# A conditional residual and paged attention on one core: written order on all engines, a queue of norms with fixed slots, and the sets in the order q01, kv, q23

## The chip, the core and the metric

The kernel runs on one core of a Trainium2 chip. The metric is the device time of one execution in microseconds; lower is better. The core has five engines, each with a queue of its own: TensorE (PE, with its weight load PEld), VectorE (DVE), ScalarE (ACT), GpSimd (POOL) and SyncE (SP). SP issues most of the DMAs, POOL the gathers of V and some stores, ACT a few stores.

## What is computed

The input x is 64 batches of 32 tokens of 512 values. All is float32.

```
W = L0_cond_weights[condition]                     # 64 x 32 x 32
x = x + einsum('bct,bcd->bdt', x, W)               # x1
q, k, v = x1 @ Wq.T, x1 @ Wk.T, x1 @ Wv.T          # 32 heads of q, 8 of k and v, 128 wide
q, k = rope(rmsnorm(q) * q_norm_w), rope(rmsnorm(k) * k_norm_w)
k_all = concat(k_cache[block_table], k)            # 512 cached rows (16 pages of 32), 32 new ones
v_all = concat(v_cache[block_table], v)
probs = softmax(mask(q @ k_all.T / sqrt(128)))     # cached rows beyond the length are masked
out = x1 + (probs @ v_all) @ Wo.T
```

## The kernel before, in words

**Tiling.** Four batches (4 x 32 = 128 tokens) make a *step*. There are 16 tiles of four batches, and the heads are taken in two halves (`hh`): steps 0 to 15 compute four key heads with their sixteen query heads, steps 16 to 31 the others. Within a step each batch `bt` has four *slots*, one for each key head `g`; slot = 4 bt + g, so a step has sixteen slots, 0 to 15. The main loop runs over steps, batches and key heads.

**What a slot holds.** `scores` (L800) multiplies the cached keys of one head by the queries of four heads (eight matmuls in L804) and ACT takes the exponential (`pr`, L815). `values` (L859) multiplies the exponentials of the slot before by V (L865); DVE adds the part of the new keys, takes the reciprocal and scales (L883 to L886), and `turn` transposes the result (L896). `head_keys` (L788) copies the keys of one head out of the loaded pages (`kh`, L797, DVE), three heads ahead; there are three `kh` tiles. `next_values` (L1266) masks one block of gathered V rows on ACT (L361) and issues a gather three blocks ahead on POOL (L348). At slot 0 `new_scores` multiplies the new keys by the queries (`psn`, L825) and ACT makes `pn` (L833); at slots 1 and 3 `new_values` multiplies `pn` by the new V (`pnv`, L849) and ACT copies it. At the start of each batch SP issues the sixteen K pages of the batch after next (L321); for the last batch of a step eight at its start (slot 12) and eight at slot 13.

**Work for later steps.** Between these, the slots carry the projections for the step after next. Steps 1 to 3 are projected plainly (`classic`). From step 4 on two steps form a *pair*, and their projections are made by a Strassen-like scheme of seven products for a *set* of weights: set 0 is q heads 0 and 1 (q01), set 1 is q heads 2 and 3 (q23), set 2 is k and v (kv). The products of a set are in four pieces (`products`, L655; the matmuls are L665, the sums on DVE L681, the first copy `z` on ACT L695), and a table `where` (L1214) gives the slots of each: for pair steps n + 2 and n + 3, set 0 in slots 4, 6, 8, 9 of step n, set 1 in slots 11 to 14 of step n, and set 2 in slots 4, 6, 8, 11 of step n + 1; n is even. Sums of weights are made once for each half (`sums_w`), stored, and loaded again (`load_sums`, L652). Each product that is a query or key head goes through `finish` to `norm_rope` (L465): a Square on ACT (L470), the mean on DVE (L474, L475), a power on POOL (L477), five DVE operations (L481 to L496), then a transpose on DVE and a store of the rows to DRAM on POOL's queue (`turn_rows`, L512 to L520). `spread` (L522) loads the rows as columns for the step that uses them: `q_cols` for batches 0 to 2, `q_last` for batch 3. `out_proj` (L736) multiplies the outputs of the step before by the output weights (L743), in four parts; `reload` and `store` bring and take the accumulated tile.

**Order.** `plan` and `ahead` are tables of work by (step, slot) and (step, batch), filled by `at`, `input_of`, `set_of`, `spread_of`, `angles_of` and `tables_of`. For PE and SP the order is the written one during the whole kernel (`manual_schedule`, L91). For DVE, ACT and POOL it is the written one until `opening.close()` (L1109); after that a planner with a cost model orders their instructions, but for those that `tc.issue_after` ties to an earlier one (L1146, L1269). The planner's order is fixed in the program; nothing is reordered at run time.

**Tiles.** The accumulated tile (`x1_a`, L375) is in tag `acc` with two buffers, or in `sums` or `u3`. `z`, `u2`, `u3`, `w1`, `w2` are single buffers of sums and norms. PSUM has two banks for scores, two for values and four for all else (`pp`).

Of the kernel before, what the change touches and what calls it, by code (L numbers as in the profile page):

```python
# [20 lines left out]
P = 128  # L21
# [38 lines left out]
def cond_resid_paged_attention_kernel(  # L60
# [148 lines left out]
    def steps_of(exact, pools):  # L209
# [165 lines left out]
        def x1_a(st):  # L375

            tag = "acc"
            if st.n in (2, 3, 5) and not exact:
                tag = "sums"
            elif st.n > 6 and st.n % 2 and not exact:  # L380
                tag = "u3"
            st.acc = work.tile(
                [P, HID], F32, tag=tag, name=f"acc_{st.name}", bufs=1 if tag[0] == "u" else 2
            )
            src = acc_d[st.t] if st.hh else x[st.t * P : (st.t + 1) * P, :]
            nc.sync.dma_start(st.acc, src)
# [31 lines left out]
        def keep_x1(st):  # L418
            nc.sync.dma_start(acc_d[st.t], st.acc)
# [12 lines left out]
        def rot_tile(st, kind):  # L432
            table = work.tile([P, 2, 2, HD], F32, tag="rot", name=f"rot_{kind}_{st.name}", bufs=2)
            st.rot[kind] = table
            return table
# [29 lines left out]
        def norm_rope(st, pp, name, kind, to=None):  # L465
# [3 lines left out]
            sq = work.tile([P, 4, D], F32, tag="w2", name=f"sq_{name}", bufs=1)  # L469
            nc.scalar.activation(  # L470
                sq.rearrange("p h d -> p (h d)"), pp, AF.Square, scale=1.0 / math.sqrt(D)
# [7 lines left out]
            r = work.tile([P, 4, 2, HD], F32, tag="w1", name=f"rope_{name}", bufs=1)  # L479
            u = work.tile([P, 4, 2, HD], F32, tag="w2", name=f"ropeu_{name}", bufs=1)  # L480
            nc.vector.tensor_tensor(  # L481
                r.rearrange("p h e f -> p h (e f)"),
                pp.rearrange("p (h d) -> p h d", h=4),
                cw.rearrange("p e f -> p (e f)").unsqueeze(1).to_broadcast([P, 4, D]),
                ALU.mult,
            )
# [23 lines left out]
        kept = []  # L510
# [24 lines left out]

        def finish(st, i, pp, name, kind):

            if by_tensor(st):
# [12 lines left out]
                norm_rope(st, pp, name, kind, to)  # L551
            else:
                turn_rows(st, i, norm_rope(st, pp, name, kind))
# [60 lines left out]
        def sums_x(pair):  # L614
            a = lambda i: pair.x[:, i].rearrange("p c q -> p (c q)")
            nc.vector.tensor_tensor(a(S1), a(A21), a(A22), ALU.add)
            nc.vector.tensor_tensor(a(S2), a(S1), a(A11), ALU.subtract)
            nc.vector.tensor_tensor(a(S4), a(A12), a(S2), ALU.subtract)
            nc.vector.tensor_tensor(a(S3), a(A11), a(A21), ALU.subtract)
# [35 lines left out]
        def products(pair, k, first):  # L655
# [46 lines left out]
            def p5_p2():  # L702
                t["c"] = bank("pc")
                product(t["c"], S1, t[1], True)
                product(t["a"], A12, t["b21"])
                done(s0, e0, t["a"])

            def p7():
                product(t["b"], S3, made[pair.hh, k][1] if first else pair.t[k, 1])
                t["u3"] = temp("u3")  # L710
                add(t["u3"], t["b"], t["z"])
                if e1[0] == "v":
                    p4 = lambda a: a.rearrange("p (g d) -> p g d", g=GH)
                    add(new_v(s1), p4(t["u3"]), p4(t["c"]))
                else:
                    add(t["u3"], t["c"], t["u3"])
                    done(s1, e1, t["u3"])

            def p4_p3():
# [4 lines left out]
                product(t["c"], S4, t["b22"])  # L724
                if e1[0] == "v":
                    p4 = lambda a: a.rearrange("p (g d) -> p g d", g=GH)
                    add(new_v(s0), p4(t["u2"]), p4(t["c"]))
                else:
                    add(t["u2"], t["c"], t["u2"])
                done(s1, e0, t["z"])  # L730
                if e1[0] != "v":
                    done(s0, e1, t["u2"])

            return p1_p6, p5_p2, p7, p4_p3
# [25 lines left out]
        def reload(st):  # L760
            st.acc = work.tile([P, HID], F32, tag="acc", name=f"res_{st.name}", bufs=2)
# [328 lines left out]
        x1_b(second)  # L1090
        head_keys(later, 0, nc.scalar)
# [17 lines left out]
        opening.close()  # L1109
# [18 lines left out]
        def input_of(st, n, load, weights, mix, turned_at):  # L1128
            at(weights[0], weights[1], lambda: load_cond_weights(st.t))
            at(load[0], load[1], lambda: x1_a(st))  # L1130
# [3 lines left out]
        def set_of(pair, k, n, slots, first):  # L1134
            for slot, work_of in zip(slots, products(pair, k, first)):
                at(n, slot, work_of)

        def spread_of(st, last_cols):
            ahead[st.n - 1, BT - 1].append(lambda: spread(st, 0, BT - 1))
            at(st.n - 1, last_cols, lambda: spread(st, BT - 1, BT))  # L1140

        def angles_of(m, n, slot):
            def angles():
                tmp = work.tile([P, 3, TRIG * HD], F32, tag="w1", name=f"ang{m}", bufs=1)
                with tc.issue_after(last["dve"]), tc.issue_after(last["act"]):
                    reduced(m * TRIG, tmp)  # L1146
                    sines(new_trig(m * TRIG), tmp)
# [28 lines left out]
        spread_of(steps[2], 14)  # L1176
        at(2, 13, lambda: spread(steps[3], 0, BT - 1))
        at(2, 14, lambda: spread(steps[3], BT - 1, BT))


        for pair in pairs:
            s0, s1 = pair.both
            n = s0.n - 2
            early, half_first = n == 2, s0.n == NT
            if early:
                at(2, 3, lambda pair=pair: pair_x(pair))
                input_of(s0, 2, (1, 15), (1, 15), 4, 5)
                input_of(s1, 2, (2, 4), (2, 2), 6, 7)
# [4 lines left out]
            elif not pair.hh:  # L1193
                at(n - 1, 12, lambda pair=pair: pair_x(pair))
                input_of(s0, n - 1, (n - 1, 9), (n - 1, 6), 12, 13)
                input_of(s1, n - 1, (n - 1, 11 if n > 4 else 12), (n - 1, 7), 14, 15)
                at(n, 1, lambda pair=pair: sums_x(pair))
# [228 lines left out]
```

## Time and profile before

| | |
|---|---|
| median of 3 runs | 2268.01 us (2267.06 to 2268.45) |
| profiled execution | 2280.09 us, span of its instructions 2278.3 us |
| mean granted TensorE clock | 0.971 |
| busy share of PE, DVE, POOL, ACT | 94%, 60%, 41%, 38% |
| moved by DMA | 478.65 MB, mean 210 GB/s |

The span runs from the first to the last instruction. A line of a profile names the engine, the line of the kernel, the operation, what is written and read (out<-in), and how often; "idle before" is the time in which the engine stood just before such an instruction, with what ended it. PEclk is the granted TensorE clock as a share of full speed.

### The profile page before, as it was taken

What the parts mean: (1) busy time and instruction counts of PE and PEld (TensorE: products, weight loads), DVE (VectorE), ACT (ScalarE), POOL (GpSimd) and SP (SyncE); (2) the same over time, 40 slices, a digit from 0 to 9 for tenths busy, and PEclk for the clock granted to TensorE, in tenths of its full rate; (3) what the DMA queues carried; (4) which work ended last, traced back from release to release, by engine and by line L of the source; (5) the groups of instructions that cost most, each with busy time, mean ns of one, the idle gap of its engine ahead of it and who ended that gap; (6) DMA issues with size and microseconds to landing.
All of it is one profiled execution on the core that took longest, in us unless ns stands there. A gap on an engine that the chain in (4) does not pass through costs nothing. (4 is left out here: it accounts for less than half of the span.)

```text
span 2278.3 us, 42030 instructions
## 1 busy us (share of the span) xinstructions
PE 2137.4 (94%) x12804; PEld 1507.2 (66%) x12804; DVE 1361.4 (60%) x3142; ACT 865.2 (38%) x1591; POOL 923.3 (41%) x1089
## 2 busy tenths in 40 slices
PE   8998898999999999999999899999999999999998
PEld 4765666676666666666666566676767667676786
DVE  5566674756657566575755646556475565757532
ACT  3533233443433424433333333343333334342452
POOL 4444353534435344353433423334343343434431
PEclk9999899999999999999999999999999999999999
DMA  8775567777677776797757887677777767777673
GB/s 242 200 192 160 175 197 209 222 217 223 192 208 225 208 223 195 209 283 236 214 180 219 237 228 220 196 220 221 216 211 211 219 200 228 216 226 222 184 223 95
DMA packets 424314, 478.65 MB, mean 210 GB/s; under 512 B 57072, under 2 KB 323696, under 8 KB 424080
## 3 DMA queue, kind: packets, MB, share of 16 engines
q1 hardware_dynamic: 366096, 291.72, 45.0%
q0 software_dynamic: 55088, 180.01, 25.9%
q10 hardware_dynamic: 2896, 4.14, 0.5%
q8 instruction: 105, 1.72, 0.3%
q14 instruction: 129, 1.06, 0.1%
HBM read 406.45 MB, written 69.21 MB: 209 GB/s over the span
## 5 line engine op out<-in xcount | busy, mean ns | idle before, releaser
L348 POOL DMA_INDIRECT raw_x<-in_vc_dram,v_row x512 | 525.1, 1026 | 775.7 <-ACT v_x L361 695.3
L815 ACT ACTIVATE pr_x<-ps_x 128x512 f32<-128x512 f32 x511 | 306.5, 600 | 917.8 <-PE ps_x L804 914.8
L865 PEld LDWEIGHTS po_x<-v_x,pr_x 128*128 128x128 f32 x4088 | 531.2, 196 | 157.2 <-issue 138.4
L865 PE MATMUL po_x<-v_x,pr_x 128*128 128x129 f32 x4088 | 563.6, 282 | 6.2 <-ACT pr_x L815 5.4
L743 PE MATMUL pout_x<-wo_x,ot_x 128*128 128x512 f32 x1024 | 464.0, 597 | 10.3 <-DMA wo_x<-in_wo_dram 10.3
L804 PE MATMUL ps_x<-q_cols_x,kh_x 128*128 128x128 f32 x3064 | 419.6, 281 | 45.3 <-DVE kh_x L797 37.7
L804 PEld LDWEIGHTS ps_x<-q_cols_x,kh_x 128*128 128x128 f32 x3064 | 386.0, 198 | 51.0 <-issue 46.3
L797 DVE COPY kh_x<-k_t_x 128x512 f32<-128x512 f32 x506 | 215.6, 433 | 295.2 <-PE ps_x L804 202.3
L361 ACT ACTIVATE v_x<-raw_x,valid 128x512 f32<-128x512 f32 x512 | 366.6, 721 | 41.0 <-DMA raw_x<-in_vc_dram,v_row 40.8
L743 PEld LDWEIGHTS pout_x<-wo_x,ot_x 128*128 128x128 f32 x1024 | 189.3, 192 | 214.5 <-issue 214.5
L477 POOL TENSOR_TENSOR rs_q_x<-ms_q_x,minus_half 128x4 f32<-128x4 f32 x128 | 144.8, 1131 | 155.2 <-DVE ms_q_x L475 154.5
L665 PE MATMUL pb_x<-t_x,x_x 128*128 128x512 f32 x432 | 203.6, 594 | 0.0
L883 DVE TENSOR_TENSOR nv_x<-po_x,nv_x 128x258 f32<-128x258 f32 x256 | 106.3, 415 | 150.8 <-PE po_x L865 143.9
L520 POOL DMA_DIRECT2D heads_d<-rows_x x150 | 122.4, 816 | 153.7 <-DVE rows_x L516 109.4
L474 DVE TENSOR_REDUCE ms_q_x<-sq_q_x 128x4 f32<-128x512 f32 x128 | 86.6, 676 | 114.9 <-ACT sq_q_x L470 113.7
L804 PE MATMUL ps_x<-q_last_x,kh_x 128*128 128x128 f32 x1024 | 136.1, 276 | 0.0
L681 DVE TENSOR_TENSOR u_x<-pb_x,z_x 128x512 f32<-128x512 f32 x84 | 57.6, 686 | 128.0 <-PE pb_x L665 94.8
L804 PEld LDWEIGHTS ps_x<-q_last_x,kh_x 128*128 128x128 f32 x1024 | 125.5, 193 | 0.0
L665 PEld LDWEIGHTS pb_x<-t_x,x_x 128*128 128x128 f32 x432 | 77.2, 192 | 71.1 <-issue 63.0
L665 PE MATMUL pa_x<-wq_x,x_x 128*128 128x512 f32 x224 | 115.1, 640 | 0.0
L886 DVE TENSOR_TENSOR o_x<-nv_x,rden 128x256 f32<-128x256 f32 x256 | 107.4, 420 | 5.1
L665 PE MATMUL pc_x<-wq_x,x_x 128*128 128x512 f32 x224 | 105.4, 593 | 0.5 <-DVE u_x L681 0.5
(180 smaller groups left out, 2033.0 us busy)
## 6 DMA issues: line engine op xcount, KB each, us to landing
k_t_x<-in_kt_dram SPq DMA_DIRECT2D x2048, 64.0 KB
t_x<-sums_d SPq DMA_DIRECT2D x108, 512.0 KB
heads_d<-rows_x POOLq DMA_DIRECT2D x150, 256.0 KB
q_cols_x<-heads_d SPq DMA_DIRECT2D x120, 240.0 KB
q_last_x<-heads_d SPq DMA_DIRECT2D x120, 80.0 KB
sums_d<-t SPq DMA_DIRECT2D x18, 512.0 KB
raw_x<-in_vc_dram,v_row POOLq DMA_INDIRECT x512
wo_x<-in_wo_dram SPq DMA_DIRECT2D x32, 256.0 KB
```

Source lines behind the costliest of these rows:

```text
L348: nc.gpsimd.indirect_dma_start(out=raw.rearrange("p g d -> p (g d)"), out_offset=None, in_=vc, in_offset=bass.IndirectOffsetOnAxis(ap=v_ro ...
L361: nc.scalar.activation(v_bufs[b % 2][:, c, :, 0:D], raw, AF.Copy, scale=ok)
L477: nc.gpsimd.tensor_tensor(rs, ms, minus_half, ALU.pow)
L520: nc.gpsimd.dma_start(heads_d[st.n][:, :, i, :].rearrange("k p c -> p k c"), part)
L665: nc.tensor.matmul(bank, pair.x[:, i, c, :], w[:, c * 512 : (c + 1) * 512], start=start and c == 0, stop=c == 1, skip_group_check=not start,)
L743: nc.tensor.matmul(st.po, st.ot[:, i, :], wt["o", st.hh, i // 4][:, i % 4, :], start=(i == 0), stop=(i == QH - 1),)
L797: last["dve"] = nc.vector.tensor_copy(k, ba.k_raw[:, :, g, :]).ins
L804: nc.tensor.matmul(ps[:, c, :], ba.k[g][:, c * P : (c + 1) * P], queries(ba, g), start=True, stop=True,)
L815: last["act"] = nc.scalar.activation(pr, ps, AF.Exp, scale=SCALE).ins
L865: nc.tensor.matmul(ba.po[:, g % 2, :], ba.pr[g][:, c, :], ba.v_t[:, c, g, :], start=(c == 0), stop=(c == VC - 1),)
L883: nc.vector.tensor_tensor(t, ba.po, t, ALU.add)
L886: nc.vector.tensor_tensor(ba.o[:, both, :], t[:, :, 0:D], rd.unsqueeze(2).to_broadcast([P, 2, D]), ALU.mult,)
```

## The change

DVE, ACT and POOL keep the written order to the end: `opening.close()` moves from the start of the main loop to its end, and the two `tc.issue_after` fall away. Since the written order now counts, several things are written elsewhere:

- **Norms.** `finish` only puts a product into `outputs_due` when it belongs to a pair. The Square is traced at the end of a slot (`square_next`) and the rest of the norm in the next one (`norm_next`), behind its scores and key copy, in fixed slots (`norm_slots`): 7, 9, 10, 11, 14 of even steps, 2, 7, 9, 10 and 14 (in the second half 12) of odd ones; in steps below 4 any slot takes one. In `norm_rope` the first DVE multiplication stands before the mean.
- **Sets.** kv takes slots 11 to 14 of step n, and q23 slots 4, 6, 8, 11 of step n + 1. In a set P3 moves from the last piece to the third, beside P7, and the sums are grouped anew. The v of the pair's second step is kept in `u3` and copied by ACT at slot 4 of step n + 1 (`late_v`).
- **Key copies.** `head_keys` stands right behind `scores` in its slot, where it stood at the slot's end.
- **Accumulated tile.** Tag `acc` has one buffer and serves step 0 and the reloads; steps 1 to 5 use `sums`, later ones `u2` or `u3` by turns. Step 1's tile is stored on POOL's queue and loaded again.
- **SP's order.** The last columns of `spread` follow the others at the start of batch 3, where they had a slot of their own; loads of x, rotation tables, query, key, value and output weights move by some slots; the final reload moves from slot 10 to 14. Rotation tables have four buffers instead of two, and `sums_x` is in two parts, at slots 2 and 3.

The core of the diff (moves of `tables_of`, `input_of` and `sums_w` by a slot or two, and the edits that only pass `sq` and `late_v` on, are left out):

```diff
-            tag = "acc"
-            if st.n in (2, 3, 5) and not exact:
-                tag = "sums"
-            elif st.n > 6 and st.n % 2 and not exact:
-                tag = "u3"
+            tag, bufs = "acc", 2 if exact else 1
+            if 0 < st.n < 6 and not exact:
+                tag, bufs = "sums", 2
+            elif st.n and not exact:
+                tag = ("u2", "u3")[st.n % 2]
...
         def finish(st, i, pp, name, kind):
 
+            outputs_due.append((st, i, pp, name, kind))
+            while outputs_due and (st.pair is None or not in_slots):
+                square_next()
+                norm_next()
+
+        def square_next():
+            if outputs_due and not squared:
+                _, _, pp, name, _ = outputs_due[0]
+                squared.append(squares(pp, name))
+
+        def norm_next():
+            if squared:
+                st, i, pp, name, kind = outputs_due.pop(0)
+                normed(st, i, pp, name, kind, squared.pop())
...
             def p5_p2():
                 t["c"] = bank("pc")
                 product(t["c"], S1, t[1], True)
+                t["u3"] = temp("u3")
+                add(t["u3"], t["c"], t["z"])
                 product(t["a"], A12, t["b21"])
                 done(s0, e0, t["a"])
 
-            def p7():
+            def p3_p7():
+                product(t["c"], S4, t["b22"])
+                if e1[0] == "v":
+                    add(new_v(s0), p4(t["u2"]), p4(t["c"]))
+                else:
+                    add(t["u2"], t["c"], t["u2"])
+                    done(s0, e1, t["u2"])
                 product(t["b"], S3, made[pair.hh, k][1] if first else pair.t[k, 1])
...
+                    add(t["u3"], t["b"], t["u3"])
+                    if e1[0] == "v":
+                        late_v.append(lambda: nc.scalar.copy(new_v(s1), p4(t["u3"])))
+                    else:
+                        done(s1, e1, t["u3"])
...
-        opening.close()
+        in_slots.append(True)
...
             ahead[st.n - 1, BT - 1].append(lambda: spread(st, 0, BT - 1))
-            at(st.n - 1, last_cols, lambda: spread(st, BT - 1, BT))
+            last = lambda: spread(st, BT - 1, BT)
+            if last_cols is None:
+                ahead[st.n - 1, BT - 1].append(last)
+            else:
+                at(st.n - 1, last_cols, last)
...
                 where = [
                     (0, n, (4, 6, 8, 9)),
-                    (1, n, (11, 12, 13, 14)),
-                    (2, n + 1, (4, 6, 8, 11)),
+                    (2, n, (11, 12, 13, 14)),
+                    (1, n + 1, (4, 6, 8, 11)),
                 ]
+                at(n + 1, 4, lambda late_v=late_v: late_v.pop()())
...
             ba, c = unfilled.pop(0)
-            with tc.issue_after(last["act"]):
-                ba.fill(c)
+            ba.fill(c)
...
-        out_parts = [{8: (0, 1), 9: (2, 3)}, {5: (0,), 7: (1,), 8: (2,), 10: (3,)}]
+        norm_slots = {
+            (0, 0): (7, 9, 10, 11, 14),
+            (1, 0): (2, 7, 9, 10, 14),
+            (0, 1): (7, 9, 10, 11, 14),
+            (1, 1): (2, 7, 9, 10, 12),
+            (0, 2): (),
+        }
+        out_parts = [{8: (0, 1), 9: (2, 3)}, {5: (0,), 7: (1,), 9: (2,), 10: (3,)}]
         second_outputs = {
-            (0, 10): (0,),
-            (1, 2): (1,),
-            (1, 4): (2,),
-            (1, 5): (3, 4),
-            (1, 6): (5, 6),
-            (1, 7): (7,),
+            (0, 8): (0,),
+            (0, 10): (1, 2),
+            (0, 12): (3,),
+            (0, 14): (4,),
+            (1, 1): (5,),
+            (1, 2): (6,),
+            (1, 3): (7,),
         }
...
                     if st.n or slot > GH:
                         scores(this, g)
+                    while copied <= min(this.n * GH + g + KH, NHH * NT * BT * GH - 1):
+                        head_keys(this if copied // GH == this.n else later, copied % GH)
+                        copied += 1
+                    if st.n < 4 or slot in norm_slots[st.n % 2, st.hh]:
+                        norm_next()
...
-                    while copied <= min(this.n * GH + g + KH, NHH * NT * BT * GH - 1):
-                        head_keys(this if copied // GH == this.n else later, copied % GH)
-                        copied += 1
+                    nn, ns = divmod(st.n * BT * GH + slot + 1, BT * GH)
+                    if nn < 4 or ns in norm_slots[nn % 2, nn // NT]:
+                        square_next()
...
         out_proj(steps[-1], slice(0, QH), in_range)
+        opening.close()
```

## The prediction, on record before the result

> **What bounds the kernel now.** I read the page's busy times and slices first, then TensorE's waits, then the places behind the longest of them.
>
> ```profile
> PE 2137.4 (94%) x12804; PEld 1507.2 (66%) x12804; DVE 1361.4 (60%) x3142; ACT 865.2 (38%) x1591; POOL 923.3 (41%) x1089
> PEclk9999899999999999999999999999999999999999
> ```
>
> TensorE (PE) is the bound, and no other engine is above 60%. The second line says that its clock is not full in any slice. So the change can only give back time in which PE stands or runs slowly. The list of TensorE's waits (us in total, times, longest us) says where it stands:
>
> ```profile
> PE ps_x L804 <- DVE kh_x L797: 37.7, 19, 4.3
> PE pnv_x L849 <- ACT pn_x L833: 35.1, 16, 2.8
> PE psn_x L825 <- DMA q_last_x<-heads_d: 12.3, 2, 9.3
> PE pout_x L743 <- DMA wo_x<-in_wo_dram: 10.3, 2, 7.2
> PE pmix_x L398 <- DMA acc_x<-in_x_dram: 10.1, 2, 8.2
> PE ps_x L804 <- DMA q_cols_x<-heads_d: 7.6, 3, 5.1
> PE po_x L865 <- ACT pr_x L815: 5.4, 11, 0.5
> ```
>
> These seven lines hold 118.5 us, all but some 15 us of what PE waits. The second and the last belong together: eleven times, at the end of an even step and the start of the odd one, PE waits 0.51 and then 2.76 us. The timeline of ScalarE at one of them:
>
> ```profile
> 1430.47 0.63 ACT L470 ACTIVATE sq_q_x<-z_x 128x512 f32<-128x512 f32 x1 [5.47 <-DVE z_x L681]
> 1431.01 0.58 ACT L815 ACTIVATE pr_x<-ps_x 128x512 f32<-128x512 f32 x1
> 1434.18 0.63 ACT L470 ACTIVATE sq_q_x<-u_x 128x512 f32<-128x512 f32 x1 [1.99 <-DVE rden L885]
> 1435.81 0.59 ACT L833 ACTIVATE pn_x<-psn_x 128x512 f32<-128x512 f32 x1
> ```
>
> A Square (L470) stands in ACT's queue before the exponentials and waits for a sum on VectorE (DVE), which is still busy with the norms of set q23; behind it wait the exponentials of the scores and of the new keys (pn). What such a stop costs beyond itself is in the windows around it (us; PE, PEld, DVE, ACT and POOL busy; clock; DMA share and GB/s):
>
> ```profile
> 1434.40:1437.50 3.10, 1.05 (x19) 0.93 (x20) 3.10 (x8) 2.48 (x5) 1.94 (x3) 1.00 0.30 85
> 1437.50:1440.90 3.40, 3.40 (x18) 3.40 (x18) 2.80 (x8) 0.00 (x0) 2.15 (x3) 0.50 0.48 154
> 1440.90:1444.30 3.40, 3.40 (x38) 3.16 (x37) 3.16 (x9) 2.69 (x8) 0.91 (x2) 1.00 0.56 169
> ```
>
> After the gap 3.4 us run at half clock: 1.7 us more. DVE is full in the first window, PE is not.
>
> The first line of the waits is at slot 4 of even steps: the key copies (kh) are late because the pages of K are. SyncE (SP) issues them late; one boundary, and SP's wait in the list of the whole run:
>
> ```profile
> 913.94 11.84 SPq L321 DMA_DIRECT2D k_t_x<-in_kt_dram  x8
> 926.44 5.58 SPq L321 DMA_DIRECT2D k_t_x<-in_kt_dram  x8
> ...
> 934.44 1.10 DVE L797 COPY kh_x<-k_t_x 128x512 f32<-128x512 f32 x3 [4.12 <-DMA k_t_x<-in_kt_dram]
> ```
>
> ```profile
> SPq L321 <- DMA x1t_d<-x_x: 41.3, 9, 10.4
> ```
>
> Eight pages take 11.84 us to issue where the next eight take 5.58, because one of them waits for the landing of a store from ACT that the code writes a slot later than these pages: the planner put it ahead.
>
> **What the Trainium skill says.** "TensorE: Matmul & The Clock Gate", section What's actually happening: the array runs at half clock after an idle window of about 3.4 us and again at full clock after a busy one of that length. The trace agrees on the half and on the 3.4 us, but here a wait of 2.76 us is enough; I use the trace. "Perfetto Trace Analysis", Sequencer Loop: an engine's instructions wait for their semaphores in the order of its queue. The Square above shows it: the exponential behind it starts at 1431.01, when the Square is done. "DMA: Bandwidth & Descriptors", Issuing engines are not separate DMA queues: transfers of SP, ACT and POOL share the same 16 engines, so a moved issue saves only issue time. The windows agree as far as they go: the share is 0.70 to 0.85 in nearly all of the run, neither free nor full.
>
> **The change part by part.** Durations are of the profiled execution: 2280.1 us with a span of 2278.3. The median is 2268.0, a factor of 0.9947; sums are made at 2280.1 and scaled at the end.
>
> *Sets in the order q01, kv, q23.* In the kernel before, each even step carries eight q norms and each odd one two k norms. A norm costs DVE 0.68 + 0.68 + 0.16 + 0.75 + 0.68 + 0.69 + 0.70 = 4.3 us, ACT one Square of 0.6, POOL a power of 1.1 and the issue of a store, 0.8. With kv in slots 11 to 14 and q23 in the odd step it is five and five, and only one norm (slot 14) stands near the boundary instead of four: 13 us less for DVE there. No Square on u or z stands before pn: the list of norm slots has neither 0 nor 1. So 11 x (2.76 + 0.51) = 36 and 11 x 1.7 = 19 go: **-54**. Next late there is the v mask's wait for its gather (ACT v<-raw, 40.8 us in 36 times in the list of waits), which today already makes the 0.2 to 2.2 us waits for pn at odd-to-even boundaries; I leave those.
>
> *Output weights of the second half earlier* (part 1 from slot (1,2) to (0,10), the last from (1,7) to (1,3)). They are first needed at slot 5 of step 17, and step 16 has freed each tile (slots 5, 7, 9, 10) before its load. The waits are 10.3 us, and the clock from 1305 to 1340 us averages 0.81: 0.19 x 35 = 6.7. Of 17 I take **-14**; the same 4 MB meet a DMA share of 0.87 there, so 0 to 17.
>
> *Spreads and input earlier in steps 2 and 3.* The last columns go from slot 14, behind sixteen K pages in SP's queue, to the start of slot 12, ahead of them; x for step 6 goes from behind eight pages to ahead of them. What that holds up: four issues of 0.45 us before the pages. Waits 12.3 + 7.6 + 10.1 = 30, and some 9 of half clock around them (clocks of 0.63, 0.70 and 0.74 over 14, 23 and 20 us, halved because part of it is idle). Of 39 I take 60%, as x now has two slots to land: **-23** (10 to 39).
>
> *K pages.* In one written order no page waits for a later store of ACT, and the key copy stands before the norm in its slot, so the K buffer is free as soon as the scores are done. Waits 37.7, and 8 of them long enough for 1.6 us of clock, 13. The boundaries without a store (second half) wait 0.5 to 2.9 us for another reason: sixteen issues of 0.55 us in seven slots of 1.8 us. That stays. Half: **-26** (0 to 51).
>
> *Written order on DVE, ACT and POOL.* What is queued behind each wait: on ACT the Square comes at the end of a slot, behind it the next exponential, wanted by PE one slot later (1.8 us at least): 0 to 2.2 us (its wait for PE pa), I take 0. On POOL the norm's power and its store of heads come before the slot's gather, so the gather leaves up to 6 us later; three are in flight, so three slots cover it: 10 us with products, only 5.4 at slots 12 to 15. There ACT's mask and the exponential behind it are late by up to 3 us. On DVE the key copy of slot 1 waits for its pages with the sums of x behind it; P6 at slot 4 wants one of these, 0 to 1 us. Below nothing no order can go by itself. I take 0.6 us at each of 28 boundaries: **+17** (0 to 60).
>
> *At nothing:* the ACT copy of v for the second step (14 of 0.58 us, ACT at 38%); P3 moved beside P7 and the sums regrouped, five per set as before, but a bank's reader is now a slot ahead; four rot tiles instead of two; one accumulator tile, as the reload at slot 3 follows the store at 13; POOL's extra store of step 1 (0.8 us) with one reload; q, k and v weights moved by a few slots with over ten to spare; ScalarE's sines at slot 5, under 3.4 us of output projection. If the cover were gone the copies would cost 8 us together.
>
> Sum: -54 - 14 - 26 - 23 + 17 = -100; 2280.1 - 100 = 2180.1; x 0.9947 = **2168.5 us**.
>
> **Rivals.** *K next late:* PE reaches slot 4 some 5 us earlier in each pair, and K becomes the pace. For: K already ends last there, and the DMA share is 0.7 to 0.85. Against: last-half pairs wait only 0.5 us. Boundaries, weights and the early part still give 91, 17 is paid, and 14 pairs pay 1.6 + 1.6 more: 91 - 17 - 45 = 29, so 2251 or **2239 us**. *Slower:* late gathers stop ACT. Place: the mask before the exponential at the boundaries; price: a 3 us gap and 1.7 of clock, 28 times, 132 instead of 17, with a gain of 117: 2295, or **2283 us**. It decides from 4.2 us a boundary. For: ACT already waits 40.8 us there. Against: the order on ACT of mask and exponential is that of today. *It changes nothing in effect:* the planner's order was nearly the written one, or new waits fill the old places: **2266 us**. Against: the Square at 1430.47 is out of written order's slot.
>
> **How the numbers follow.** The forecast 0.68 (2130 to 2210), K next late 0.17 (2210 to 2250), slower 0.08, no effect 0.04, better than 2130 0.03 (all of K and the early waits gone: 2119 to 2130). The range 2130 to 2242 holds the first and three quarters of the second: 0.8. Faster by over 0.2% (about what a measurement of this kernel can tell): 0.88; within it 0.04; slower 0.08.
>
> **What would show it.** In the changed kernel's waits, pnv<-pn falls from 35 to under 8 us and po<-pr to near 0; pout<-wo is gone; ps<-kh falls to about 20; the clock rises from 0.971 to about 0.985; SP's wait for x1t_d is gone. Even and odd steps have equal counts of row transposes (L516). It is wrong if ACT's waits for raw grow by tens of us, or if ps<-kh grows.

## The result and the profile after

The changed kernel takes 2243.98 us (median of 4 runs, 2234.52 to 2248.9) against 2268.23 of the kernel before on the same chip: a ratio of 0.9882 with a 95% interval of 0.9841 to 0.9923. It is faster, by about 27 us by this ratio (24 by the medians) where the forecast had 100, and lies 2 us above the forecast's range. The profiled run took 2247.31 us with a span of 2245.5; the one of before had a span of 2278.3.

From the page of the kernel after, the busy times (share of the span, instructions) and the slices of TensorE's clock:

```profile
PE 2118.6 (94%) x12804; PEld 1491.4 (66%) x12804; DVE 1420.8 (63%) x3142; ACT 879.6 (39%) x1604; POOL 910.5 (41%) x1090
...
PEclk9999988999999999999999999999999999999999
```

TensorE works as many matmuls and is still the bound. It is busy for 19 us less and stands 14 us less. By the table below, 12 of the 19 us are less work at half clock; the other 7 no run takes apart. Its longest waits in the kernel after (us in total, times, longest us):

```profile
PE ps_x L828 <- DVE rot_q_x L444: 21.2, 4, 5.8
PE pnv_x L873 <- ACT pn_x L857: 17.6, 7, 5.2
PE po_x L889 <- ACT pr_x L839: 13.3, 9, 4.1
PE ps_x L828 <- DVE kh_x L821: 11.6, 4, 5.6
PE pc_x L687 <- DVE u_x L703: 8.9, 2, 8.4
PE pp_q_x L458 <- ACT x1t_x L409: 8.5, 1, 8.5
PE px1t_x L404 <- DVE acc_x L397: 6.5, 3, 3.1
PE ps_x L828 <- DMA q_cols_x<-heads_d: 5.5, 1, 5.5
```

The waits for wo, acc and q_last, 33 us before, have left the top of this list (1.7 us are left of acc and 1.5 of q_last). The wait for pn is halved, not gone. Keys have kept theirs under another name: the first line waits at L828 (scores) for a table piece (L444) that stands on VectorE right behind a late key copy, as a timeline shows below. With the fourth line that is 33 us, against 37.7 before. Grown are po (5.4 us before), pc (0.5) and px1t (1.8).

Where in the run the time went is seen when both traces are cut into steps, at the first matmul of each step's own new scores. For each group: its span, and in brackets what TensorE stands before a matmul and what half clock costs while it works, in us. The 6.5 us or so after the last matmul are in neither.

```
steps          before               after
start to 1     171.5 (12.2,  1.7)   176.2 (14.0,  4.8)
2 to 4         259.7 (28.2,  8.6)   265.7 (29.6, 11.7)
odd 5 to 13    327.6 (18.3,  6.7)   298.2 ( 1.5,  0.0)
even 6 to 12   301.5 (15.5,  8.0)   306.2 (21.2,  7.2)
14             79.2  ( 6.3,  2.6)   86.2  (13.0,  2.1)
15, 16         141.2 ( 8.7,  3.4)   137.0 ( 7.7,  1.7)
17             77.7  (13.4,  6.3)   64.9  ( 4.8,  2.5)
even 18 to 28  431.4 (10.6,  3.4)   440.4 (18.0,  5.9)
odd 19 to 29   375.6 (19.8, 10.2)   350.8 ( 5.1,  0.0)
30, 31         112.7 ( 1.0,  0.0)   119.9 ( 5.3,  3.0)
all            2278.1               2245.5
```

The odd steps, which begin with the even-to-odd boundaries, gave 29.4 + 24.8 = 54 us, step 17 another 13 and steps 15 and 16 another 4. Steps up to 4, the even steps 6 to 14 and 18 to 28, and the end took 39 of it back. One trace of each kernel is compared here and below; groups that an edit can't touch differ by up to 5 us between traces (steps 30 and 31 take 115.3 us in experiment 1), so differences of that size say little. Three places in the trace of after show by what.

**Late keys.** The boundary of steps 5 and 6 in the kernel after, where step 6 begins at 501.7. First the timeline of ScalarE (start, us, what):

```profile
495.87 0.33 ACTq L414 DMA_DIRECT2D x1t_d<-x_x  x1
...
500.68 0.33 ACTq L414 DMA_DIRECT2D x1t_d<-x_x  x1
```

Then that of SyncE:

```profile
499.96 0.34 SPq L674 DMA_DIRECT2D t_x<-sums_d  x1
501.62 7.43 SPq L321 DMA_DIRECT2D k_t_x<-in_kt_dram  x8
509.09 0.43 SPq L780 DMA_DIRECT2D acc_d<-res_x  x1
509.71 3.95 SPq L321 DMA_DIRECT2D k_t_x<-in_kt_dram  x8
```

And that of VectorE, with the idle time before in brackets:

```profile
515.52 0.43 DVE L821 COPY kh_x<-k_t_x 128x512 f32<-128x512 f32 x1 [10.30 <-DMA k_t_x<-in_kt_dram]
515.87 0.22 DVE L444 SCALAR_TENSOR_TENSOR rot_q_x<-norm_q,trig_x 128x64 f32<-128x64 f32 x1
```

SyncE's load of sums goes out at 499.96, when the store that ScalarE issued at 495.87 has landed; then one of eight pages waits for the second store, issued at 500.68, so that eight pages take 7.43 us and the next eight 3.95. Nothing in the code orders these: in the trace the issues of SyncE and ScalarE take their landing semaphores from one round of eight, and the load and the page come to those (105 and 100) that the two stores still hold. The key copy is idle for 10.30 us and TensorE stands 5.17 us, up to 516.10. SyncE's waits for such stores in the whole run of after come to 58 us (56 before); the longest lines:

```profile
SPq L674 <- DMA x1t_d<-x_x: 26.5, 4, 7.3
...
SPq L321 <- DMA x1t_d<-x1t_x: 14.6, 3, 7.6
...
SPq L530 <- DMA x1t_d<-x_x: 6.8, 1, 6.8
```

**A sum in place.** Step 14 of the kernel after, first SyncE's timeline:

```profile
1073.81 8.66 SPq L321 DMA_DIRECT2D k_t_x<-in_kt_dram  x16
1082.52 0.91 SPq L665 DMA_DIRECT2D sums_d<-t  x2
```

Then VectorE's:

```profile
1085.37 1.23 DVE L667 TENSOR_TENSOR t<-wq_x,t 128x1024 f32<-128x1024 f32 x1 [15.86 <-DMA sums_d<-t]
```

The subtraction at L667 overwrites the tile that is just being stored. The store stands behind sixteen K pages in SyncE's queue, and in written order VectorE stands with it, 15.86 us. There are three such places, one in step 3 and one each in steps 14 and 15, with 37.5 us of VectorE together; TensorE stands 8.4 us behind the first and 3.1 behind this one.

**Late gathers.** The boundary of steps 25 and 26 in the kernel after, first POOL's timeline:

```profile
1857.91 1.15 POOL L485 TENSOR_TENSOR rs_q_x<-ms_q_x,minus_half 128x4 f32<-128x4 f32 x1 [1.73 <-DVE ms_q_x L483]
1861.05 0.83 POOL L521 DMA_DIRECT2D heads_d<-rows_x  x1 [1.99 <-DVE rows_x L517]
1862.18 1.04 POOL L348 DMA_INDIRECT raw_x<-in_vc_dram,v_row  x1 [0.31 <-issue]
```

Then ScalarE's:

```profile
1867.76 0.72 ACT L361 ACTIVATE v_x<-raw_x,valid 128x512 f32<-128x512 f32 x1 [4.27 <-DMA raw_x<-in_vc_dram,v_row]
1868.39 0.58 ACT L839 ACTIVATE pr_x<-ps_x 128x512 f32<-128x512 f32 x1
1868.87 0.59 ACT L857 ACTIVATE pn_x<-psn_x 128x512 f32<-128x512 f32 x1
```

The gather of slot 12 leaves after the norm's power and store, the mask (L361) waits 4.27 us for gathered rows, and both exponentials behind it are late: TensorE stands 2.77 us for pn. ScalarE's wait for raw in the whole run of the kernel before:

```profile
ACT v_x L361 <- DMA raw_x<-in_vc_dram,v_row: 40.8, 36, 3.6
```

And of the kernel after:

```profile
ACT v_x L361 <- DMA raw_x<-in_vc_dram,v_row: 166.9, 86, 7.2
```

### The profile page after: what moved, and what is told of

Same layout as the page of the kernel before. It is cut to its first block, busy times and chain, and to the rows that moved or that the text cites. A ratio compares the mean times of both kernels' runs of the same rounds, so it can differ in the third digit from the quotient of the medians.

```text
span 2245.5 us, 42014 instructions
## 1 busy us (share of the span) xinstructions
PE 2118.6 (94%) x12804; PEld 1491.4 (66%) x12804; DVE 1420.8 (63%) x3142; ACT 879.6 (39%) x1604; POOL 910.5 (41%) x1090
## 4 chain that ended last, share of the span: by engine, by line
PE 70%; DMA 10%; DVE 5%; issue 5%; SPq 4%; POOL 3%; ACT 1%; DVEq 0%; POOLq 0%; ACTq 0%
PE pout_x L767 16%; PE po_x L889 15%; PE ps_x L828 15%; PE pb_x L687 8%; PE pc_x L687 6%; PE pa_x L687 6%; SPq L321 3%; DMA k_t_x<-in_kt_dram 3%; DMA raw_x<-in_vc_dram,v_row 3%; PE pp_q_x L458 1%; DMA t_x<-sums_d 1%; PE pnv_x L873 1%; POOL raw_x L348 1%; POOL rs_q_x L485 1%; PE psn_x L849 1%
## 5 line engine op out<-in xcount | busy, mean ns | idle before, releaser
L348 POOL DMA_INDIRECT raw_x<-in_vc_dram,v_row x512 | 517.7, 1011 | 458.8 <-ACT v_x L361 348.0
L889 PE MATMUL po_x<-v_x,pr_x 128*128 128x129 f32 x4088 | 560.5, 281 | 19.0 <-ACT pr_x L839 13.3
L767 PE MATMUL pout_x<-wo_x,ot_x 128*128 128x512 f32 x1024 | 459.4, 592 | 0.0
L828 PE MATMUL ps_x<-q_cols_x,kh_x 128*128 128x128 f32 x3064 | 417.2, 280 | 42.1 <-DVE rot_q_x L444 21.2
L361 ACT ACTIVATE v_x<-raw_x,valid 128x512 f32<-128x512 f32 x512 | 365.8, 718 | 171.3 <-DMA raw_x<-in_vc_dram,v_row 166.9
L828 PEld LDWEIGHTS ps_x<-q_cols_x,kh_x 128*128 128x128 f32 x3064 | 384.3, 197 | 45.4 <-issue 44.6
L485 POOL TENSOR_TENSOR rs_q_x<-ms_q_x,minus_half 128x4 f32<-128x4 f32 x128 | 142.6, 1114 | 334.2 <-DVE ms_q_x L483 333.4
L828 PE MATMUL ps_x<-q_last_x,kh_x 128*128 128x128 f32 x1024 | 136.0, 276 | 0.0
L828 PEld LDWEIGHTS ps_x<-q_last_x,kh_x 128*128 128x128 f32 x1024 | 125.5, 193 | 0.0
L687 PE MATMUL pa_x<-wq_x,x_x 128*128 128x512 f32 x224 | 110.4, 617 | 0.0
L497 DVE TENSOR_TENSOR rope_q_x<-rope_q_x,rs_q_x 128x512 f32<-128x512 f32 x120 | 83.1, 692 | 27.0 <-POOL rs_q_x L485 16.1
L495 DVE TENSOR_TENSOR rope_q_x<-rope_q_x,ropeu_q_x 128x512 f32<-128x512 f32 x128 | 88.6, 692 | 4.4
```

The source lines that it names most:

```text
L348: nc.gpsimd.indirect_dma_start(out=raw.rearrange("p g d -> p (g d)"), out_offset=None, in_=vc, in_offset=bass.IndirectOffsetOnAxis(ap=v_ro ...
L361: nc.scalar.activation(v_bufs[b % 2][:, c, :, 0:D], raw, AF.Copy, scale=ok)
L485: nc.gpsimd.tensor_tensor(rs, ms, minus_half, ALU.pow)
L687: nc.tensor.matmul(bank, pair.x[:, i, c, :], w[:, c * 512 : (c + 1) * 512], start=start and c == 0, stop=c == 1, skip_group_check=not start,)
L767: nc.tensor.matmul(st.po, st.ot[:, i, :], wt["o", st.hh, i // 4][:, i % 4, :], start=(i == 0), stop=(i == QH - 1),)
L828: nc.tensor.matmul(ps[:, c, :], ba.k[g][:, c * P : (c + 1) * P], queries(ba, g), start=True, stop=True,)
```

## Experiments

Ratios are to the kernel before, measured beside each experiment on the same chip, with their 95% intervals; times are medians. "To after" is the quotient of two such ratios. In the fences of edits, "-" is the kernel that is edited.

**1. The turned input stored by POOL** (in the changed kernel)

```
-                keep_x1t(st, nc.scalar)
+                keep_x1t(st, nc.gpsimd)
```

> The changed kernel, with the store of the turned input (x1t_d) issued by POOL instead of ACT. Theory A: K pages are late in four first-half pairs because SP's issues wait for the landing of ACT's store (6.6 and 3.4 us at 496 to 506 us), whatever order the code is written in. Then TensorE's wait ps<-rot_q at L444 (21.2 us in 4 times), which is really that for kh, goes, with some 7 us of half clock: 2244 - 28 = 2216 us, at least 15 us less than the changed kernel, and SP's waits for x1t_d fall from 33 us to under 5. Rival B: the pages are late because sixteen issues of 0.5 us don't fit in the slots before the key copy; the waits stay or take another name, and the time is within 6 us of 2244. Rival C: POOL's issue of 0.8 us makes a norm's power or a gather late, and part of the gain comes back as pn or v<-raw waits: 2230.

Measured: 2211.9 us, 0.9741 (0.9717 to 0.9765), so 0.986 to after, 32 us less. TensorE's waits for keys in this kernel, and the sixteen pages of the same boundary:

```profile
PE ps_x L828 <- DVE kh_x L821: 11.0, 5, 7.1
...
PE ps_x L828 <- DVE rot_q_x L444: 4.3, 3, 3.1
```

```profile
494.62 9.04 SPq L321 DMA_DIRECT2D k_t_x<-in_kt_dram  x16
```

The wait that bore the table's name falls from 21.2 to 4.3 us, SyncE's waits for x1t_d are gone, and sixteen pages now go out in one piece. The even steps 6 to 12 fall from 306.2 to 283.8 us, with no half clock left in them; steps 2 to 4 fall by 10. Theory A holds. The pages can be issued fast enough (B falls), and no wait of the kind that C named grows by more than a few us: TensorE's for pn is 10.0 us after 17.6, ScalarE's for raw 173 after 167 (C falls).

**2. The sums of weights stored by POOL** (in the changed kernel)

```
             for i, t in enumerate(made[hh, k]):
-                nc.sync.dma_start(sums_d[hh][k][:, i, :], t)
+                nc.gpsimd.dma_start(sums_d[hh][k][:, i, :], t)
```

> The changed kernel, with the two stores of sums of weights (sums_d, both issued ahead of the in-place subtraction at L667) on POOL's queue instead of SP's, where they stand behind sixteen K pages. Theory A: VectorE's 37.5 us of waiting at L667 (3 times, up to 15.9) is a cost of the written order that the forecast left out; it falls under 8 us, and TensorE's waits behind it (8.4 at pc<-u, 3.1, some of ps<-q_cols) go with their half clock: 15 to 20 us less than the changed kernel, some 2227 us. Rival B: VectorE has slack there and TensorE waits next for K or for queries at the same places: less than 5 us.

Measured: 2237.56 us, 0.9837 (0.9816 to 0.9859). VectorE's wait in this kernel:

```profile
DVE t L667 <- DMA sums_d<-t: 16.1, 5, 4.5
```

37.5 us become 16.1: the store no longer stands behind pages, but its landing still has to be waited for. Steps 2 to 4 fall from 265.7 to 257.4 us in the trace, steps 14 and 15 don't change. That is half of what A expected. The ratio to after is 0.995, and the two intervals overlap, so the time alone doesn't show the gain; the trace does, for step 3.

**3. Mask and gather ahead of the norm** (in the changed kernel, from step 4 on, in norm slots from 4)

```
+                    if first_gather:
+                        fill_next()
                     if st.n < 4 or slot in norm_slots[st.n % 2, st.hh]:
                         norm_next()
```

> The changed kernel, with the slot's V mask on ACT and its gather on POOL written ahead of the norm in the slots that have one (from step 4 on, slots 4 to 15). Theory A: the norm's power and store on POOL make the gathers late at the boundaries, and ACT's mask with the exponential behind it: ACT's wait v<-raw falls from 167 us in 86 times to under 90, TensorE's pnv<-pn and po<-pr from 31 us to under 15: 12 to 20 us less than the changed kernel, some 2228 us. Rival B: the gathers are late because the transfers are slow there, whatever the order of their issue: v<-raw stays over 140 us and the time within 5 us. Rival C: the mask now stands before the exponential's slot and stops ACT a slot earlier: slower by 5 to 20 us.

Measured: 2231.8 us, 0.9829 (0.9805 to 0.9853), 0.995 to after or 12 us less, of which the two intervals leave little certain; TensorE's waits say more:

```profile
PE po_x L889 <- ACT pr_x L839: 2.8, 1, 2.8
PE pnv_x L873 <- ACT pn_x L857: 2.7, 4, 1.6
```

They were 13.3 and 17.6 us. The even steps 18 to 28 fall by 8.5 us (by 4 in experiment 1, which doesn't touch them); step 16 gives 7 back. ScalarE's wait for raw falls only to 124.6 us, not under 90: half of A's number was wrong, though what it was to bring came. So most of ScalarE's waiting there stopped nobody.

**4. The planner instead of the written order** (in the changed kernel: the opening's fixed order ends where it did in the kernel before; the two `tc.issue_after` of that kernel are not put back)

```
         in_slots.append(True)
+        opening.close()
...
         out_proj(steps[-1], slice(0, QH), in_range)
-        opening.close()
```

> The changed kernel with its tables, queues and order of sets, but the planner orders the engines again after the opening, as in the kernel before. Theory A: the sets' order is what gave the boundaries their 55 us, and the written order by itself costs 20 to 40 us (the in-place sum, late gathers, late K pages): 2205 to 2225 us. Rival B: the written order gave the boundaries their gain, because the planner puts Squares before exponentials whatever the order of sets: 2260 to 2300 us, with pnv<-pn back at over 25 us.

Measured: 2307.42 us, 1.0165 (1.0135 to 1.0195): slower than the kernel before. The first of TensorE's waits here:

```profile
PE po_x L889 <- ACT pr_x L839: 49.6, 27, 3.6
PE ps_x L828 <- DVE kh_x L821: 32.9, 12, 6.2
```

The two halves of the run differ. The odd steps 19 to 29 take 345.9 us with 1.4 of standing (375.6 with 19.8 before): there the changed order of sets and the norm slots bring all of the gain without the written order. The odd steps 5 to 13 take 346.6 us with 32.3 of standing. But TensorE's old wait, for pn, is in neither half. What stands ahead of the late exponentials in steps 5 to 11 is the sine of the rotation angles (L156) with two table loads; ScalarE's timeline at the start of step 5:

```profile
457.05 1.28 ACT L156 ACT_TABLE_LOAD   x1
...
458.67 1.28 ACT L839 ACT_TABLE_LOAD   x1
459.97 1.08 ACT L839 ACTIVATE pr_x<-ps_x 128x512 f32<-128x512 f32 x2
```

Later in these steps TensorE waits 4.7 us for a sum of x that stands behind a norm on VectorE. In even steps of the second half the exponentials stand behind masks that wait for gathered V rows; in the whole run ScalarE waits 340 us for these (167 in the changed kernel). Sines and masks are what the two `tc.issue_after` of the kernel before held back. So A is right about the boundaries of the second half and wrong in the total, and B has the sign but not the reason. What the planner costs with these ties in place no run shows.

**5. Edits 1, 2 and 3 together** (in the changed kernel)

```
-                keep_x1t(st, nc.scalar)
+                keep_x1t(st, nc.gpsimd)
...
-                nc.sync.dma_start(sums_d[hh][k][:, i, :], t)
+                nc.gpsimd.dma_start(sums_d[hh][k][:, i, :], t)
...
+                    if first_gather:
+                        fill_next()
```

> The changed kernel with three edits together: x1t_d stored from POOL, the stores of the sums of weights from POOL, mask and gather ahead of the norm in the slots that have one. Theory A: they hit different places (K in the first half, the sums in steps 3, 14 and 15, boundaries of the second half), so their ratios to the changed kernel multiply: 0.986 x 0.995 x 0.995 = 0.976, 2190 us. Rival B: they meet, since what one frees the next wait takes up (POOL gets more issues and the gathers come late again, or K is the next at each boundary): 2205 us or more. Then TensorE's waits for pr, kh or q_cols are over 25 us.

Measured: 2190.44 us, 0.9632 (0.9617 to 0.9646), as the product has it. To kernel 1 that is 0.989, with intervals apart: edits 2 and 3 together are worth some 25 us. The page:

```profile
PE 2101.0 (96%) x12804; PEld 1475.7 (67%) x12804; DVE 1420.6 (65%) x3142; ACT 878.8 (40%) x1604; POOL 936.5 (43%) x1117
...
PEclk9999999999999999999999999999999999999999
```

The slices at 8 are gone. By steps: 2 to 4 take 246.0 us (before 259.7), the odd ones 5 to 13 take 296.4 and 19 to 29 take 354.8, the even ones 6 to 12 take 281.5 and 18 to 28 take 431.6, and step 17 takes 66.9.

**6. No norm slots** (in the changed kernel: the line that begins the queue is taken out, so each Square and norm is written where its product is)

```
-        in_slots.append(True)
```

> The changed kernel without the fixed norm slots: each output's Square and norm are written at once where its product is written; order of sets, tables and written order as changed. Theory A: the order of sets alone takes the norms from the boundary (only the last k norm is near it, at slot 14), so the odd steps 5 to 13 keep their 298 us with gaps under 8 us, and the time is within 15 us of 2244. Rival B: the slots matter: a Square written right behind its product stops ACT ahead of the slot's exponential, and four norms at slots 8 and 9 stop VectorE ahead of key copies: TensorE's gaps grow by 30 us or more, 2280 to 2330 us.

Measured: 2323.09 us, 1.0214 (1.0197 to 1.0232), 75 us more than after. The first of TensorE's waits:

```profile
PE pb_x L687 <- DVE u_x L703: 48.5, 28, 4.3
```

The bank of P6 and P7 waits for a sum on VectorE, 28 times, twice in each pair; in the trace a whole norm of about 4.5 us stands ahead of that sum. Theory B holds for the even steps 6 to 12 (306.2 to 334.2 us). The odd ones 5 to 13 go to 308.3 only, of 327.6 before, and those from 19 to 29 to 361.3, of 375.6: some 60% of the 54 us comes with the order of sets in written order, and the rest with the slots.

**7. The turned input stored by POOL in the kernel before** (the same line as in 1)

> The kernel before, with the store of the turned input (x1t_d) issued by POOL instead of ACT, and nothing else changed. Theory A: K pages of the kernel before wait for the landing of these stores too, so ps<-kh falls from 37.7 us to under 20 and SP's wait for x1t_d (41.3 us) goes: 15 to 30 us less than before, 2240 to 2255. This is what the forecast's K step wanted from the written order. Rival B: under the planner the pages that come earlier only move the wait to pn at the boundary and to the gathers: within 6 us of before.

Measured: 2255.97 us, 0.992 (0.9903 to 0.9937), 18 us less than before. Three of TensorE's waits in this kernel:

```profile
PE pnv_x L849 <- ACT pn_x L833: 40.0, 18, 2.8
PE ps_x L804 <- DVE kh_x L797: 23.8, 16, 4.6
PE psn_x L825 <- DMA q_last_x<-heads_d: 11.1, 2, 7.9
```

Keys fall from 37.7 to 23.8 us, the even steps 6 to 12 from 301.5 to 282.2, and little else moves. SyncE's waits for x1t_d are gone. Theory A holds in the gain, at its lower end (the wait for keys stays above the 20 us that it named): the late pages were there before the change, for the same reason, and their gain could be had without it.

**8. Spreads and input at their later places** (in kernel 5: the spreads of steps 2 to 4, and x for steps 6 and 7 behind eight pages; the edits for step 4 and for x are left out of the fence)

```
-        spread_of(steps[2], None)
-        spread_of(steps[3], None)
+        spread_of(steps[2], 14)
+        at(2, 13, lambda: spread(steps[3], 0, BT - 1))
+        at(2, 14, lambda: spread(steps[3], BT - 1, BT))
```

> The kernel with the three edits (e5, 2190 us), with the spreads of steps 2, 3 and 4 and the loads of x for steps 6 and 7 back at their later places, behind the K pages. Theory A: the early places are worth what the forecast gave them (-23), and the new waits of steps 2 and 3 only covered it; undoing them brings back TensorE's waits for q_last, q_cols and acc (30 us in the kernel before, 7 after): 2205 to 2215 us. Rival B: in written order the early places are worth little, since the same transfers only wait elsewhere: within 5 us of 2190.

Measured: 2208.86 us, 0.973 (0.9711 to 0.9749), 1.010 to kernel 5 or 22 us more (18 by the medians), and in the trace 20 of them are in steps 2 to 4 (246.0 to 266.5). The old waits are back:

```profile
PE psn_x L849 <- DMA q_last_x<-heads_d: 10.4, 2, 5.9
...
PE ps_x L828 <- DMA q_cols_x<-heads_d: 6.3, 3, 4.3
...
PE pmix_x L396 <- DMA acc_x<-in_x_dram: 4.9, 1, 4.9
```

Theory A holds: the early places are worth some 20 us once nothing else stands in the same steps.

**9. POOL's stores of the sums right behind the sums** (in kernel 5: the two stores move from the set's first part to the slot of the sums)

```
             made[hh, k] = t2, t3
+            for i, t in enumerate(made[hh, k]):
+                nc.gpsimd.dma_start(sums_d[hh][k][:, i, :], t)
...
-            for i, t in enumerate(made[hh, k]):
-                nc.gpsimd.dma_start(sums_d[hh][k][:, i, :], t)
```

> The kernel with the three edits (e5, 2190 us), with POOL's stores of the sums of weights written right behind the sums instead of a slot or two later. Theory A: VectorE's 17 us of waiting at L667 falls to under 5, TensorE's 6.7 us at pc<-u go with some clock: 2180 to 2187 us. Rival B: POOL waits for the sums with gathers and powers queued behind it, or K is next late: 2188 us or more.

Measured: 2181.35 us, 0.9622 (0.9597 to 0.9646). The interval covers that of kernel 5, so it is not shown to be faster. VectorE's wait at L667 is down from 17.0 to 4.4 us and TensorE's for pc from 6.7 to 2.4, as A expected; but two thirds of the trace's 15 us lie in steps with no such sum. It is beside 5 the fastest version here.

**10. The key copy at the end of its slot** (in kernel 5)

```
-                    while copied <= min(this.n * GH + g + KH, NHH * NT * BT * GH - 1):
-                        head_keys(this if copied // GH == this.n else later, copied % GH)
-                        copied += 1
                     def fill_next():
...
                         turned = []
+                    while copied <= min(this.n * GH + g + KH, NHH * NT * BT * GH - 1):
+                        head_keys(this if copied // GH == this.n else later, copied % GH)
+                        copied += 1
                     nn, ns = divmod(st.n * BT * GH + slot + 1, BT * GH)
```

> The kernel with the three edits (e5, 2190 us), with the key copy at the end of its slot, behind the norm, as in the kernel before. Theory A: the key copy's place ahead of the norm is part of the K gain; behind a norm of 4.3 us the copies come late where slots are short, and TensorE's waits for kh and rot_q (14 us) grow by 10 us or more: 2200 to 2215 us. Rival B: the copy is written three slots ahead of its use and this covers it: within 5 us of 2190.

Measured: 2240.02 us, 0.9872 (0.9847 to 0.9897), 1.025 to kernel 5, 50 us more. VectorE's timeline at the end of step 19 of this kernel:

```profile
1437.91 0.68 DVE L475 TENSOR_TENSOR rope_q_x<-z_x,rot_q_x 128x512 f32<-128x512 f32 x1
...
1442.71 0.71 DVE L517 STREAM_TRANSPOSE rows_x<-rope_q_x 128x512 f32<-128x512 f32 x1
...
1444.31 0.45 DVE L821 COPY kh_x<-k_t_x 128x512 f32<-128x512 f32 x1
```

And TensorE's first wait in it:

```profile
PE ps_x L828 <- DVE kh_x L821: 57.6, 26, 5.6
```

The copy starts 6.4 us after the norm began, TensorE waits 2.98 us for it at 1444.91, and this comes again in each pair of the second half; the odd steps 19 to 29 and the even ones 6 to 12 grow by 18 us each. The three slots of lead don't cover a norm; B falls, and A's 10 us were too few by far.

## Why the forecast was wrong

The sign was right; three terms of the sum were not.

- **Sets in the order q01, kv, q23: -54, came.** The odd steps fell by 54 us and their half clock is gone. The reason given, that no Square stands before pn at these boundaries, holds: the wait for pn is gone from them under the planner (experiment 4) and, with 1.0 us left in the whole run, without the norm slots (6), and these two and the changed kernel have the order of sets in common. The slots are the smaller part: without them some 40% of the 54 is lost and the even steps lose more. That the sum is met to the us is partly luck: 31 us of it are less standing and 17 half clock, where the forecast had 36 and 19, 6 are neither, and step 17, one of its eleven boundaries, is not among them.
- **Output weights: -14, came.** The 10.3 us of waits are gone, and step 17 is 12.8 us shorter; its boundary is a part of that.
- **Spreads and input: -23, came and was covered.** TensorE's waits for q_last, q_cols and acc fell from 30 to 9 us, yet steps up to 4 grew by 11. The step took the old waits for the whole of those steps. New ones stood there: the sum in place (8 us, experiment 2) and a store of x1t_d (10, experiment 1). Experiment 8 shows some 20 us once they are gone.
- **K pages: -26, failed.** The sentence that fails is "In one written order no page waits for a later store of ACT". I took the wait for one of order in the code. It is a wait for a landing, and written order changed only which issue meets it: SyncE's load of sums and a page instead of a page. SyncE's waits for x1t_d stayed (56 us before, 58 after), and TensorE's for keys, under both names, fell from 37.7 us to 33 only. Experiment 7 shows 18 us of it in the kernel before, experiment 1 32 us in the kernel after. The second half of the step, the key copy ahead of the norm, holds, and is worth 50 us (10), but against a written order without it and not against the planner's.
- **Written order: +17, too small by a term that is missing.** Late gathers, for which I took 0.6 us at each boundary, cost some 12 us (3), within the 17. Their place is the one that the first step left as it was: at the starts of the even steps TensorE's waits for pn grew from 5 to 18 us. But the sum in place was not priced at all: I asked of each moved instruction what it waits for, and not of the one that stays in its place and overwrites what SyncE has still to store. With it the two are worth 25 us (kernel 5 against kernel 1).
- **At nothing:** the copies of v and the tables don't appear in TensorE's waits by themselves; the wait of px1t for the accumulated tile's sum grew from 1.8 to 6.5 us, and no run takes it apart. Step 14 is 7 us longer than before, with a key copy late by some 5 us also in kernels 5 and 9; what makes it late stays open. (In the trace of after, eight pages take 8.89 us to issue ahead of it, from 1048.45, between loads of the second half's query weights that the change put in these slots.)

By the table, -23 became +11 (start to step 4) and -26 became +5 (even steps 6 to 12); the 9 us more in the even steps 18 to 28 come mostly with the late pn. With edits 1, 2 and 3 the trace is 88 us shorter than before, of the 100 that the forecast summed; the store is worth 32 of what was missing and the other two some 25. Of the rivals, "K next late" gave 2239 us, near the time, but for another reason: not the pace of the issues at all 14 pairs, but a wait for a store at four of them. Of what was to show the forecast wrong, ScalarE's wait for raw did grow by tens of us; that was the right place to look and only a small part of the cause. Of the waits and the clock that were to show it right, only the end of the wait for wo came in full: pn stands at 17.6 us and not under 8, po at 13.3, the keys at 33 and not 20, and the clock at 0.975 and not 0.985. Two readings of the forecast were wrong and changed no term: a 9 in the clock's slices is 90% or more, so it doesn't say that the clock is not full (it is 1.00 from 57 to 171 us), and the DMA share is under 0.70 in 9 of 38 windows of 60 us.

## What to carry to other kernels

A wait of a DMA queue for another queue's transfer need not come from the order of the code: see which landing it waits for, and move the store to a queue that doesn't share it, before the order is changed for it. When a fixed order takes the place of a planner, look on each engine for instructions that wait long for something slow (here an overwrite of a tile that is still being stored, and a mask for a gather) and see who is queued behind them. A planner doesn't hide these by itself: in experiment 4 ScalarE waits more for gathers than in any other run here, and TensorE 16.3 us for the overwrite. A gain in a stretch is only a gain if nothing new stands in the same stretch, so it is priced by stretch and not by the name of the wait.

## What the runs showed of the hardware

- The Trainium skill, "DMA: Bandwidth & Descriptors", Issuing engines are not separate DMA queues, says that starting transfers from several engines saves only the sequencer's time for the issue, usually little. Here an issue of 0.33 us (L414), moved from ScalarE to POOL, saves 32 us. What it saves is not issue time but a wait that the section does not speak of: SyncE's next issue had waited up to 7.6 us for that store's landing. In the traces SyncE and ScalarE use the same eight landing semaphores (100 to 107) and POOL eight others (109 to 116). The measurement decides.
- Half clock goes by windows of a fixed grid, and not by the length of a gap. In each of the twelve traces here every stretch of half clock begins on one grid of 3.413 us. With the traces cut on it from 14 us on, TensorE's busy share of each window at full clock says what follows (the ends of matmuls are modelled, so the shares are estimates): all 176 windows under 43% were followed by half clock, and of the 7243 over 48% only three. So a stop costs more or not by where it falls. Two of nearly one length in the kernel after, of 2.72 us up to 1606.3 and of 2.77 us up to 1869.5, with the window behind the second (columns as in the forecast):

```profile
1604.70:1608.11 3.41, 1.81 (x26) 1.69 (x27) 0.00 (x0) 3.41 (x9) 1.92 (x3) 1.00 1.09 349
1867.53:1870.94 3.41, 1.43 (x22) 1.28 (x22) 0.00 (x0) 2.43 (x5) 0.94 (x1) 1.00 1.00 335
1870.94:1874.35 3.41, 3.41 (x18) 3.38 (x16) 1.08 (x3) 2.33 (x7) 1.16 (x2) 0.50 0.75 230
```

The first leaves TensorE busy for 53% of its window and costs nothing more; the second leaves 42%, and the next 3.4 us run at half clock. The section of the skill on the clock gate, cited in the forecast, speaks of an idle window of about 3.4 us: the length agrees with the grid, but a window that is busy for up to 43% was enough here.
